# Two bottleneck layers in fp32: order of work at the two borders, in the middle stage and at the ends of the fused stage

## The chip, the cores and the metric

The kernel runs on one core of one Trainium2 chip. The metric is the device time of one execution in microseconds (us), as the median of several runs. One execution is profiled as well; its time is given beside the others.

## The reference

Two layers of the same form follow each other, on x of 64 x 1024 x 14 x 14 in fp32. Each is a bottleneck of three convolutions (1024 to 256 channels by 1x1, 256 to 256 by 3x3, 256 to 1024 by 1x1), each followed by a batch norm with the statistics of the batch, and closed by a scaled residual and a relu:

```python
def _bn(x, gamma, beta):
    mean = jnp.mean(x, axis=(0, 2, 3), keepdims=True)
    var = jnp.var(x, axis=(0, 2, 3), keepdims=True)
    xn = (x - mean) * jax.lax.rsqrt(var + EPS)
    return gamma.reshape(1, -1, 1, 1) * xn + beta.reshape(1, -1, 1, 1)

def layer(x, w1, b1, g1, be1, w2, b2, g2, be2, w3, b3, g3, be3, residual_scale):
    out = jax.nn.relu(_bn(_conv(x, w1, b1, 1, 0), g1, be1))
    out = jax.nn.relu(_bn(_conv(out, w2, b2, 1, 1), g2, be2))
    out = _bn(_conv(out, w3, b3, 1, 0), g3, be3)
    out = jax.nn.softplus(residual_scale)[0] * out
    return jax.nn.relu(x + out)
```

The second layer takes the first one's result.

## The kernel before

**Tiles.** The 64 images are cut into T = 32 tiles of two images, 392 columns each (`PX`). Channels lie on the 128 partitions: a tile of x has 8 slots (`CS`), a tile of the 256 inner channels has 2 (`MS`).

**Products.** A 1x1 convolution is cut into 2 x 2 blocks and done with seven products instead of eight (class `Seven`, with `Conv1`, `Conv3` and `Direct` for the three uses). `p1` to `p7` are the products on TensorE, and `after1` to `after7` what ScalarE and VectorE do with each. The products of one unit run between those of its neighbours (`stream`, `direct_stream`). `p4` is added onto the bank of `p1`, `p6` and `p7`, once ScalarE has copied it (`au<-ay`); `p5` and `p3` share a bank. The 3x3 convolution takes the rows and columns of the image through small transforms, so that TensorE sees the products `m<-sums`, `l<-diffs`, `columns<-sums` and `columns<-v`.

**Stages**, as the timeline shows them: conv1 of layer 0 until about 300 us, a border, conv2 of layer 0 until 580, a middle stage ("mixed") until 790, the fused stage until 1234, a border, conv2 of layer 1 until 1500, statistics (gram) until 1565, and the final stage until the end.

**Border.** A batch norm needs the statistics of all tiles, so the last results of conv1, the scale and shift, the norm of the first image rows and the first transform of conv2 follow each other. `Conv1.closing` writes this order by hand. The border of layer 0 has two tiles left in it (`two_tiles`), that of layer 1 one. `border.steps(n)` issues the next n steps of `first_combination` for slot 1 and then slot 0: on VectorE `r<-t` (line 854), `sums<-r` (782), `diffs<-r` (804) and `v<-r` (796), on ScalarE the edge copies of v; after them `steps<-y` (884) serves the next transform. `border.affine_of` makes `mv`, `minus`, the reciprocal, scale and shift.

**Mixed.** It computes conv3 of layer 0 for the statistics and keeps the results of the later tiles, unscaled, as z. `first()` does one tile in eight single products; after them `direct_stream` runs 60 units of seven products. In one step of a unit stands one product of its own or of the unit before. The results of a unit's second row are `kept<-cp,cu` (618, of `p7`) and `kept<-cy,kept` (612, of `p3`), and `finish` takes the second row's `bn_stats` (626) and stores z by SyncE's queue. Beside this, the inner tensor is normed (ScalarE, 128x320 columns at a time), centered (VectorE, `y<-y,minus_c`, 1506), and moved ("home", SyncE's queue) into another layout, in five pieces; the tables `moves` and the conditions on `unit` set when.

**Fused.** conv3 of layer 0 for half of the tiles and conv1 of layer 1 run between each other. For the other half (odd places p) `kept_rows` loads rows of z, scales them and adds them to x: on VectorE in one instruction (`x<-y,scale,x` or `x<-whole,scale,x`, 1906), or on GpSimd in two (1892 and 1893). A relu on ScalarE follows each row, and a store of the whole tile the last (`rest`). The last place, p = 31, stands right before the border of layer 1. `begun` is the list of what is left over from the tile before: two relus and the store of that tile.

**Order.** Instructions run in each engine's order of issue, which the hand-written loops set. DMAs are issued by SyncE (SP), ScalarE (ACT) and GpSimd (POOL), each with a queue of its own.

Of the kernel before, what the change touches and what calls it, by code (L numbers as in the profile page):

```python
# [18 lines left out]
CS = C // P  # L19
# [22 lines left out]
ROWS = 5 * CS, 13 * CS  # L42
AHEAD = 8


# [24 lines left out]
def bottlenecks(ctx: ExitStack, tc: tile.TileContext, x, w1s, w2s, w3s, pars, out):  # L70
# [272 lines left out]
    class Conv1(Seven):  # L343
# [34 lines left out]
        def bank(self, tag):  # L378

            if self.border is not None and tag == "x":  # L380
                return self.psum.tile(self.n, "ap" if len(self.ts) > 1 else "cx")
            return self.psum.tile(self.n, self.prefix + ("y" if self.border is not None and tag == "p" else tag))

# [7 lines left out]
        def closing(self, before):  # L391

            border = self.border

            yield from self.p1()
            for s in range(MS):
                summarize(self.stats[:, s : s + 1], T // 2 - 1, T - 2 * len(self.ts), PX)
            yield from before.p4()  # L400
            yield from self.p6()
            yield from self.p5()
            yield from self.p7()

            two_tiles = len(self.ts) > 1
            between = itertools.chain(*((before.p3(), before.p2()) if two_tiles else (before.p2(), before.p3())))
            yield from itertools.islice(between, CS // 4)
            yield from self.p4()
            border.affine_of(1)
            border.norm(1)  # L410
            yield from between
            border.begin()
            border.steps(3)
            if two_tiles:
                border.steps(2)
                yield from self.p2()
                border.steps(2)
                yield from self.p3()
            else:
                yield from self.p2()  # L420
                yield from self.p3()
            border.affine_of(0, lambda: border.steps(1 if two_tiles else 2))
            border.norm(0)
            border.steps(1 if two_tiles else 4)

# [202 lines left out]
    def direct_stream(units, between, finish):  # L628
# [3 lines left out]
        for k, now in enumerate(units):  # L632
            old = before and (before.p3, before.p7, before.p4)
            for step, part in enumerate((now.p1, *(old or (None, None))[:2], now.p5, now.p2, now.p6, old and old[2])):
                if step == 1 and earlier is not None:
                    earlier.finish()
                if part:
                    for _ in part():
                        pass
                if step == 2 and before is not None:  # L640
                    before.stat(0)
                yield k, step
# [66 lines left out]
    def conv2(b, par, aff, early, rest):  # L709
# [120 lines left out]
        def first_combination(x, s, t):  # L830
# [8 lines left out]
            for tiles in slice(0, 2), slice(2, full):  # L839
                run(stt(t[:, tiles], two_rows(0, s)[:, tiles, 0], -4.0, two_rows(0, s)[:, tiles, 1]))  # L840
            yield
            run(nc.vector.tensor_add(ra, t1, t2))
# [14 lines left out]
            yield  # L857
            x.subtract_columns(slice(1, 2), here)
            yield
            x.step_columns(slice(1, 2), here)  # L860
            yield

# [627 lines left out]
    def mixed(psum, pool, one, x_right, x_left, aff, minus_c, w3, made_c, summed_c, summed_a, mv3, xs, coming_x):  # L1490
# [92 lines left out]
        def first():  # L1583
# [8 lines left out]
            for i, (q, row) in enumerate(itertools.product(range(CS // 2), range(2))):  # L1592
# [9 lines left out]
                if i == 0:  # L1602
                    for _ in itertools.chain(summed_c, prepare(t + 1), itertools.islice(coming[t + 2], MS)):
                        pass
                if 1 < i < 6:
                    next(norms)
# [49 lines left out]
        moves = {}  # L1656
        for k, begin in enumerate((3, 13, 20, 28), 1):
            for i in range(8):
                moves[begin + i] = moves.get(begin + i, ()) + ((k, i // 2, (i % 2 * 2, i % 2 * 2 + 1)),)
        at = list(range(9, 48, 3))  # L1660
        at_first, _ = beds((None, None))
# [26 lines left out]
        for unit, step in stream:  # L1688
# [8 lines left out]
            if step == 3:  # L1697
                if q < 2 and t + 1 < T:
                    next(coming[t + 1], None)
                if 0 < unit <= 32 and unit % 2 == 0:  # L1700
                    center((unit - 1) // 8 + 1, (unit - 1) % 8 // 2)
                for where in moves.get(unit, ()):
# [91 lines left out]
    def residual(psum, xt, b, t, w3, aff, made=(), later=None):  # L1794
# [4 lines left out]
        for o in range(CS):  # L1799
# [10 lines left out]
            if (o + 1) % step == 0:  # L1810
                queue = nc.scalar if o + 1 == CS and (tail or b == 0) else nc.gpsimd if step == CS else nc.sync
                store = partial(
# [35 lines left out]
    def fused(psum, pool, one, right, coming, xs, raw, w1, w3, aff, par, stats, border, begun):  # L1848
# [34 lines left out]
        def kept_rows():  # L1883
# [13 lines left out]
            for r, (p, o) in enumerate(itertools.product(range(1, T, 2), range(CS))):  # L1897
# [3 lines left out]
                v, z = row(r, p, o)  # L1901
                if o % 2 and (p, o) not in ((T - 1, CS - 3), (T - 1, CS - 1)):
                    if p > 1 or o == CS - 1:
# [5 lines left out]
                later.append(partial(rest, v, p, o))  # L1909
                if len(later) > 2:  # L1910
                    later.pop(0)()
# [7 lines left out]
        def rest(v, p, o):  # L1919
            act(v, v, AF.Relu, bias=shift[:, o : o + 1])  # L1920
            if o == CS - 1:
                nc.scalar.dma_start(out=mids[places[p]], in_=xs[p].rearrange("p s f -> p (s f)"))

        whole = []
        pinned.append(True)
        a, c, rows = stream(first_convs(), T), stream(last_convs(), (KEPT - 1) * CS // 2), kept_rows()
        done, ended = LAG, None
        for i in range(LAG):
            next(c)
            if i == 2:  # L1930
                for late in begun:
                    late()
            if i % 2 == 1:
                next(rows)
        for k in itertools.count():
# [9 lines left out]
            late = k - 28 * (T - 4)  # L1945
            if (late >= 30 and late % 5 == 0) if late >= 20 else k % 7 == 3:
                next(rows, None)
# [333 lines left out]
```

## Time and profile before

| | before |
|---|---|
| median of 3 runs | 1893.97 us (1893.84 to 1894.53) |
| profiled execution | 1893.4 us |
| its span | 1891.4 us |
| TensorE, busy | 1872.2 us, 99% |
| VectorE, busy | 1575.9 us, 83% |
| ScalarE, busy | 1098.2 us, 58% |
| GpSimd, busy | 741.9 us, 39% |
| HBM | 228 GB/s over the span |

In timeline rows stand the start, the duration, the engine, the line, the operation with what it writes and reads, the count, and in brackets how long the engine was idle before it and what ended that. PE is TensorE, PEld its weight load, DVE VectorE, ACT ScalarE, POOL GpSimd, SP SyncE. In rows of waits stand who waited, for whom, the total, the number of times and the longest. Where a tile's name has a number (x_31), it tells which tile.

### The profile page before, as it was taken

What the parts mean: (1) busy time and instruction counts of PE and PEld (TensorE: products, weight loads), DVE (VectorE), ACT (ScalarE), POOL (GpSimd) and SP (SyncE); (2) the same over time, 40 slices, a digit from 0 to 9 for tenths busy, and PEclk for the clock granted to TensorE, in tenths of its full rate; (3) what the DMA queues carried; (4) which work ended last, traced back from release to release, by engine and by line L of the source; (5) the groups of instructions that cost most, each with busy time, mean ns of one, the idle gap of its engine ahead of it and who ended that gap; (6) DMA issues with size and microseconds to landing.
All of it is one profiled execution on the core that took longest, in us unless ns stands there. A gap on an engine that the chain in (4) does not pass through costs nothing.

```text
span 1891.4 us, 28568 instructions
## 1 busy us (share of the span) xinstructions
PE 1872.2 (99%) x9772; PEld 1560.4 (83%) x9772; DVE 1575.9 (83%) x2488; ACT 1098.2 (58%) x2287; POOL 741.9 (39%) x758
## 2 busy tenths in 40 slices
PE   9999999999999999999999999999999999999999
PEld 5555557999997998899999999989999987555555
DVE  5787867999998777788878788799999986888886
ACT  2222214677777665555555555457777792666666
POOL 0111100221205645377776776401121151666665
PEclk9999999999999999999999999999999999999999
DMA  7777644797865555778778899458788467799997
GB/s 288 272 252 271 216 181 138 203 219 214 207 205 160 181 175 206 252 270 310 271 282 309 284 299 285 195 171 222 211 208 226 143 161 292 263 341 336 358 344 271
DMA packets 262369, 458.19 MB, mean 242 GB/s; under 512 B 59152, under 2 KB 228976, under 8 KB 249040
## 3 DMA queue, kind: packets, MB, share of 16 engines
q1 hardware_dynamic: 224160, 373.28, 59.1%
q0 software_dynamic: 31216, 28.81, 7.9%
q10 hardware_dynamic: 6848, 54.28, 7.1%
q8 instruction: 78, 1.28, 0.3%
q14 instruction: 67, 0.55, 0.1%
HBM read 289.44 MB, written 141.03 MB: 228 GB/s over the span
## 4 chain that ended last, share of the span: by engine, by line
PE 91%; DVE 4%; ACT 2%; DMA 1%; issue 1%; POOL 1%; ACTq 0%; DVEq 0%; POOLq 0%
PE ay L159 20%; PE cy L159 16%; PE columns L159 13%; PE ap L159 11%; PE cp L159 10%; PE m L159 6%; PE l L159 6%; PE cx L159 5%; PE ax L159 4%; PE ps L159 1%; DMA w<-in_w 1%; ACT y L334 0%; ACT kept L334 0%; DVE y L751 0%; DVE f L1003 0%
## 5 line engine op out<-in xcount | busy, mean ns | idle before, releaser
L334 ACT ACTIVATE x<-x,shift 128x392 f32<-128x392 f32 x452 | 260.1, 614 | 79.0 <-DVE x L535 31.7
L159 PE MATMUL columns<-v,ub 128*128 128x224 f32 (+1 forms) x1536 | 302.7, 338 | 1.3 <-ACT columns L334 0.8
L159 PEld LDWEIGHTS columns<-v,ub 128*128 128x128 f32 x1536 | 268.6, 188 | 7.7 <-ACT columns L334 1.5
L334 ACT ACTIVATE cu<-cy,scale 128x196 f32<-128x196 f32 (+1 forms) x360 | 175.7, 500 | 166.6 <-PE cy L159 159.2
L159 PE MATMUL ay<-at,ws 128*128 128x196 f32 (+1 forms) x768 | 192.6, 382 | 0.5 <-ACT y L334 0.5
L159 PEld LDWEIGHTS ay<-at,ws 128*128 128x128 f32 x768 | 136.2, 190 | 35.3 <-issue 0.7
L535 DVE SCALAR_TENSOR_TENSOR x<-cp,scale,x 128x196 f32<-128x196 f32 (+1 forms) x240 | 124.6, 519 | 46.0 <-PE cp L159 44.5
L666 POOL TENSOR_TENSOR x<-x,cu 128x392 f32<-128x392 f32 x120 | 125.6, 1048 | 73.2 <-DVE x L535 72.3
L334 ACT ACTIVATE au<-ay 128x196 f32<-128x196 f32 (+1 forms) x139 | 53.6, 386 | 169.6 <-PE ay L159 158.3
L159 PE MATMUL l<-diffs,ub 128*128 128x224 f32 (+1 forms) x768 | 149.6, 337 | 0.3 <-issue 0.3
L159 PE MATMUL m<-sums,ua 128*128 128x224 f32 (+1 forms) x752 | 146.0, 336 | 0.4 <-issue 0.2
L159 PEld LDWEIGHTS l<-diffs,ub 128*128 128x128 f32 x768 | 134.6, 189 | 1.3 <-issue 0.7
L1104 POOL DMA_DIRECT2D y<-f x24 | 32.2, 1644 | 257.3 <-DVE f L1003 257.3
L159 PEld LDWEIGHTS m<-sums,ua 128*128 128x128 f32 x752 | 131.4, 189 | 1.7 <-issue 0.6
L558 POOL TENSOR_TENSOR x<-x,cu 128x196 f32<-128x196 f32 (+1 forms) x120 | 105.0, 875 | 47.5 <-ACT cu L334 19.8
L159 PE MATMUL cx<-y,w 128*128 128x196 f32 (+1 forms) x396 | 122.2, 394 | 1.1 <-ACT cx L334 1.1
L159 PE MATMUL cy<-y,w 128*128 128x196 f32 (+1 forms) x374 | 117.2, 401 | 0.9 <-DVE y L1570 0.8
L563 POOL TENSOR_TENSOR x<-x,cu 128x392 f32<-128x392 f32 x60 | 79.4, 1323 | 85.2 <-DVE x L535 80.9
L334 ACT ACTIVATE y<-y,shift,scale 128x320 f32<-128x320 f32 (+9 forms) x98 | 107.8, 1121 | 8.3 <-DVE shift L2033 7.0
L206 POOL DMA_DIRECT2D u<-y x48 | 26.0, 544 | 211.1 <-ACT y L334 210.4
L1892 POOL TENSOR_SCALAR y<-y,scale 128x392 f32<-128x392 f32 x57 | 92.4, 1621 | 29.0 <-DVE scale L2224 28.2
L626 DVE BATCH_NORM_STATS2 stats<-kept 128x6 f32<-128x392 f32 x120 | 67.4, 562 | 42.8 <-ACT kept L334 41.5
(314 smaller groups left out, 4556.8 us busy)
## 6 DMA issues: line engine op xcount, KB each, us to landing
ub<-u SPq DMA_DIRECT2D x92, 768.0 KB, 5.6
x<-in_x SPq DMA_DIRECT2D x35, 1568.0 KB, 8.5
mid<-x ACTq DMA_DIRECT2D x32, 1568.0 KB, 8.3
x<-mid SPq DMA_DIRECT2D x32, 1568.0 KB, 8.9
out<-x SPq DMA_DIRECT2D x123, 392.0 KB, 7.1
x<-in_x SPq DMA_DIRECT2D x108, 392.0 KB, 7.8
ua<-u SPq DMA_DIRECT2D x92, 256.0 KB, 3.2
z<-kept SPq DMA_DIRECT2D x60, 392.0 KB, 2.9
```

Of the source, the lines that this page charges most:

```text
L159: tc.keep_in_program_order(nc.tensor.matmul(*args, **kw))
L206: nc.gpsimd.dma_start(out=us[b][i][:, s, o], in_=u)
L334: tc.keep_in_program_order(nc.scalar.activation(*args, **kw))
L535: run(nc.vector.scalar_tensor_tensor(v, bank, self.scale[:, o : o + 1], v, ALU.mult, ALU.add))
L558: run(nc.gpsimd.tensor_add(self.part(1, 1), self.part(1, 1), u3))
L563: run(nc.gpsimd.tensor_add(v, v, self.u12))
L626: run(nc.vector.bn_stats(self.stats[:, self.o[row], self.t - KEPT, :], self.z[:, row]))
L666: nc.gpsimd.tensor_add(v, v, self.u12[:, i * self.n : (i + 1) * self.n])
L1104: nc.gpsimd.dma_start(out=out_rows[3][:, o], in_=fa[:, o, :full], accum_op=ALU.add)
L1892: run(nc.gpsimd.tensor_scalar(z, z, scale[:, o : o + 1], None, ALU.mult))
```

## The change

It reorders work at five places and changes no arithmetic.

1. *Border of both layers.* The second half of slot 1's first combination (`r<-t`, `sums<-r`, and what follows) comes behind shift instead of ahead of the last result. Between `minus` and the reciprocal only one step is left or none; the last `v<-r` of slot 1 is done together with that of slot 0, and `diffs<-r` of slot 1 between the two `steps<-y` of slot 0.
2. *Border of layer 1.* The fifth product has its own bank (cp) in place of one of y's, and the fourth product comes directly behind the seventh, where four matmuls of `ax` stood between.
3. *Mixed.* One of the four norm pairs of `first()`, with its centers and moves, goes into the stream's units 1 to 4, and later norms and centers shift by one pair. `finish` (the second row's `bn_stats` and the store of z) moves from step 1 to step 3, behind the two results of that row.
4. *Start of fused.* The two leftover relus are issued apart, and the store goes from ScalarE's queue to SyncE's.
5. *End of fused.* The rows of p = 31 follow a table of times; row 3 goes from GpSimd to VectorE, three rows come ahead of a sum, and the last tile's store is cut in two.

The diff, cut to its core:

```diff
+ROW_TIMES = 30, 35, 40, 46, 46, 46, 49, 51, 53, 55, 57, 58, 61, 65, 67
...
-            if self.border is not None and tag == "x":
-                return self.psum.tile(self.n, "ap" if len(self.ts) > 1 else "cx")
-            return self.psum.tile(self.n, self.prefix + ("y" if self.border is not None and tag == "p" else tag))
+            if self.border is not None and tag in "xp":
+                own = dict(x="ap", p="ay") if len(self.ts) > 1 else dict(x="cx", p="cp")
+                return self.psum.tile(self.n, own[tag])
+            return self.psum.tile(self.n, self.prefix + tag)
...
-            yield from itertools.islice(between, CS // 4)
+            if two_tiles:
+                yield from itertools.islice(between, CS // 4)
             yield from self.p4()
             border.affine_of(1)
             border.norm(1)
             yield from between
             border.begin()
-            border.steps(3)
-            if two_tiles:
-                border.steps(2)
-                yield from self.p2()
-                border.steps(2)
-                yield from self.p3()
-            else:
-                yield from self.p2()
-                yield from self.p3()
-            border.affine_of(0, lambda: border.steps(1 if two_tiles else 2))
+            border.steps(5 if two_tiles else 3)
+            yield from self.p2()
+            yield from self.p3()
+            border.affine_of(0, lambda: border.steps(0 if two_tiles else 1))
             border.norm(0)
-            border.steps(1 if two_tiles else 4)
+            border.steps(2 if two_tiles else 3)
...
-                if step == 1 and earlier is not None:
+                if step == 3 and earlier is not None:
                     earlier.finish()
...
                 run(stt(t[:, tiles], two_rows(0, s)[:, tiles, 0], -4.0, two_rows(0, s)[:, tiles, 1]))
+                if s == 0 and tiles.start == 0:
+                    x.subtract_columns(slice(1, 2), slice(1, 2))
...
-            x.subtract_columns(slice(1, 2), here)
-            yield
-            x.step_columns(slice(1, 2), here)
-            yield
+            if s == 0:
+                x.subtract_columns(slice(1, 2), here)
+                x.step_columns(slice(1, 2))
...
-                if 1 < i < 6:
+                if 1 < i < 5:
                     next(norms)
...
-        for k, begin in enumerate((3, 13, 20, 28), 1):
+        for k, begin in enumerate((5, 13, 20, 28), 1):
...
+        for i in range(2):
+            moves[3 + i] = ((0, 3, (i * 2, i * 2 + 1)),)
...
-                if 0 < unit <= 32 and unit % 2 == 0:
-                    center((unit - 1) // 8 + 1, (unit - 1) % 8 // 2)
+                if 0 < unit <= 34 and unit % 2 == 0:
+                    center((unit + 5) // 8, (unit + 5) % 8 // 2)
...
-                queue = nc.scalar if o + 1 == CS and (tail or b == 0) else nc.gpsimd if step == CS else nc.sync
+                queue = nc.scalar if o + 1 == CS and tail else nc.gpsimd if step == CS and b else nc.sync
...
-                if o % 2 and (p, o) not in ((T - 1, CS - 3), (T - 1, CS - 1)):
+                if (p, o) == (T - 1, CS - 2):
+                    while later:
+                        later.pop(0)()
+                        yield
+                if o % 2 and (p < T - 1 or o < 3):
...
-                if len(later) > 2:
+                if len(later) > 2 and (p < T - 1 or o < 3):
                     later.pop(0)()
...
             if i == 2:
-                for late in begun:
-                    late()
+                begun.pop(0)()
+            if i == 4:
+                while begun:
+                    begun.pop(0)()
...
-            if (late >= 30 and late % 5 == 0) if late >= 20 else k % 7 == 3:
+            for _ in range(at_end[late] if late >= 20 else k % 7 == 3):
                 next(rows, None)
```

In the border of layer 0, VectorE had this order at the last result (`y<-ay`; `au_1282` is its copy by ScalarE), with slot 1's sums ahead of it and `diffs<-r` between `minus` and the reciprocal:

```order
L437 SCALAR_TENSOR_TENSOR y<-ap,par_161,au_1246 128x14x28
L440 BN_STATS stats_0_128<-y 128x6
L854 TENSOR_TENSOR r<-t 128x448
L782 TENSOR_TENSOR sums<-r 128x224
L437 SCALAR_TENSOR_TENSOR y<-ay,par_161,au_1282 128x14x28
L440 BN_STATS stats_0_128<-y 128x6
L1985 BN_AGGR mv<-stats_0_128 128x2
L2002 TENSOR_SCALAR v<-mv 128x1
L2011 TENSOR_SCALAR minus<-mv 128x1
L804 TENSOR_TENSOR diffs<-r 128x224
```

Now it has this one there:

```order
L434 SCALAR_TENSOR_TENSOR y<-ay,par_161,au_1282 128x14x28
L437 BN_STATS stats_0_128<-y 128x6
L1995 BN_AGGR mv<-stats_0_128 128x2
L2012 TENSOR_SCALAR v<-mv 128x1
L2021 TENSOR_SCALAR minus<-mv 128x1
L2023 RECIPROCAL r<-sd 128x1
L2033 SCALAR_TENSOR_TENSOR q<-v,r 128x1
L2034 TENSOR_TENSOR rg<-r,par_161 128x1
L2035 SCALAR_TENSOR_TENSOR scale<-q,rg 128x1
L2043 SCALAR_TENSOR_TENSOR shift<-scale,minus,par_161 128x1
L853 TENSOR_TENSOR r<-t 128x448
L779 TENSOR_TENSOR sums<-r 128x224
```

`r<-t` and `sums<-r` moved from two rows ahead of `y<-ay` to behind shift; `diffs<-r` lies further on.

In a unit of mixed's stream, VectorE had the second row's statistics between the center pair and the two results:

```order
L1298 STREAM_TRANSPOSE zt_3625<-home 128x2x256
L1506 TENSOR_SCALAR y<-y,minus_c 128x320 x2
L626 BN_STATS stats_3507<-kept 128x6
L618 TENSOR_TENSOR kept<-cp,cu_4159 128x196
L612 TENSOR_TENSOR kept<-cy,kept 128x196
L626 BN_STATS stats_3507<-kept 128x6
L1298 STREAM_TRANSPOSE zt_3623<-home 128x2x256
```

Now both rows' statistics stand together, behind the results:

```order
L1296 STREAM_TRANSPOSE zt_3613<-home 128x2x256
L1504 TENSOR_SCALAR y<-y,minus_c 128x320 x2
L615 TENSOR_TENSOR kept<-cp,cu_4089 128x196
L609 TENSOR_TENSOR kept<-cy,kept 128x196
L623 BN_STATS stats_3504<-kept 128x6 x2
L615 TENSOR_TENSOR kept<-ay,cu_4118 128x196
L609 TENSOR_TENSOR kept<-ay,kept 128x196
L623 BN_STATS stats_3504<-kept 128x6 x2
L1296 STREAM_TRANSPOSE zt_3614<-home 128x2x256
```

The first `bn_stats` of each unit (of the row before) moved past the results of lines 618 and 612 (now 615 and 609).

At the end of fused, VectorE had two rows of x_31 behind the sums of x_15, and one more behind the statistics:

```order
L437 SCALAR_TENSOR_TENSOR y<-ax,par_163,au_9094 128x7x28
L454 TENSOR_TENSOR at_9172<-x_15_8817 128x784
L437 SCALAR_TENSOR_TENSOR y<-ap,par_163,au_9168 128x7x28
L456 TENSOR_TENSOR at_9171<-at_9172,x_15_8817 128x784
L457 TENSOR_TENSOR at_9170<-x_15_8817 128x784
L1906 SCALAR_TENSOR_TENSOR x_31_8939<-whole,scale,x_31_8939 128x392 x2
L440 BN_STATS stats_1_5568<-y 128x6
L1906 SCALAR_TENSOR_TENSOR x_31_8939<-whole,scale,x_31_8939 128x392
L437 SCALAR_TENSOR_TENSOR y<-ap,par_163,au_9140 128x7x28
L1970 BN_AGGR part<-stats_1_5568 128x2
```

Now three stand ahead of the sums, and one behind:

```order
L434 SCALAR_TENSOR_TENSOR y<-ax,par_163,au_9091 128x7x28
L1910 SCALAR_TENSOR_TENSOR x_31_8936<-whole,scale,x_31_8936 128x392 x3
L451 TENSOR_TENSOR at_9169<-x_15_8814 128x784
L434 SCALAR_TENSOR_TENSOR y<-ap,par_163,au_9165 128x7x28
L453 TENSOR_TENSOR at_9168<-at_9169,x_15_8814 128x784
L454 TENSOR_TENSOR at_9167<-x_15_8814 128x784
L437 BN_STATS stats_1_5565<-y 128x6
L1910 SCALAR_TENSOR_TENSOR x_31_8936<-whole,scale,x_31_8936 128x392
L434 SCALAR_TENSOR_TENSOR y<-ap,par_163,au_9137 128x7x28
L1980 BN_AGGR part<-stats_1_5565 128x2
```

Two rows of x_31 fewer stand between the sums and the second `y<-ap`, and GpSimd's two instructions for row 3 are gone.

More of the change, by code (lines that the diff above doesn't have):

```diff
@@ L1920, in rest @@
             act(v, v, AF.Relu, bias=shift[:, o : o + 1])
-            if o == CS - 1:
-                nc.scalar.dma_start(out=mids[places[p]], in_=xs[p].rearrange("p s f -> p (s f)"))
+            a = (0, CS - 2)[p == T - 1 and o == CS - 1]
+            if o == CS - 1 or p == T - 1 and o == CS - 3:
+                nc.scalar.dma_start(
+                    out=mids[places[p]][:, a * PX : (o + 1) * PX], in_=xs[p][:, a : o + 1].rearrange("p s f -> p (s f)")
+                )
         whole = []
@@ L1927, in fused @@
         done, ended = LAG, None
+        at_end = collections.Counter(ROW_TIMES)
         for i in range(LAG):
```

## The prediction

> **What bounds the kernel now.** I read the page first, then the chain of waits, then who keeps PE waiting, then the timeline at each place that the diff touches.
>
> ```profile
> span 1891.4 us, 28568 instructions
> PE 1872.2 (99%) x9772; PEld 1560.4 (83%) x9772; DVE 1575.9 (83%) x2488; ACT 1098.2 (58%) x2287; POOL 741.9 (39%) x758
> PE 91%; DVE 4%; ACT 2%; DMA 1%; issue 1%; POOL 1%; ACTq 0%; DVEq 0%; POOLq 0%
> ```
>
> PE is busy for 99% of the span and carries 91% of the chain. The change removes no matmul, so all it can win is PE's waiting; the rest of the span is fixed. Where PE waits at the places touched stands in the waits of PE, grouped by who ends them (total us, times, longest), and in the waiters of line 612:
>
> ```profile
> PE columns L159 <- DVE sums L782: 3.2, 3, 1.7
> PE cy L159 <- DVE kept L612: 2.0, 3, 0.7
> PE cy L159 <- ACT cu L334: 1.3, 3, 0.9
> PE cx L159 <- ACT cx L334: 1.1, 1, 1.1
> PE ap L159 <- DVE y L437: 1.1, 1, 1.1
>   PEld cy L159: 1.8, 4
> ```
>
> 3.2 + 2.0 + 1.3 + 1.1 + 1.1 = 8.7 us, and 1.8 of weight loads, is nearly all there is to win. The sum is made against the profiled execution, 1893.4 us: a span of 1891.4 and 2.0 around it. The median of the runs, 1893.97, lies 0.57 above it.
>
> **Border of layer 0 (two tiles).** The timeline between conv1 and conv2:
>
> ```profile
> 301.11 2.80 PE L159 MATMUL ay<-x,ws 128*128 128x392 f32 x8
> 303.72 0.61 DVE L854 TENSOR_TENSOR r<-t 128x448 f32<-128x448 f32 x1
> 304.67 0.62 DVE L437 SCALAR_TENSOR_TENSOR y<-ay,par,au 128x392 f32<-128x392 f32 x1
> 311.33 1.78 PE L159 MATMUL columns<-sums,ua 128*128 128x224 f32 x8 [1.72 <-DVE sums L782]
> 313.23 0.55 DVE L796 TENSOR_TENSOR v<-r 128x384 f32<-128x384 f32 x1
> 313.70 2.95 DVE L884 TENSOR_TENSOR steps<-y 128x2688 f32<-128x2688 f32 x1
> 319.33 1.41 PE L159 MATMUL m<-sums,ua 128*128 128x168 f32 x8 [0.20 <-DVE sums L782]
> 320.96 1.35 DVE L796 TENSOR_TENSOR v<-r 128x1152 f32<-128x1152 f32 x1
> ```
>
> The last result, y<-ay, starts at 304.67 though its product ends at 303.91, because r<-t and sums<-r of slot 1 stand ahead of it on DVE. Behind it follow the last statistics, scale, shift, the norm and the sums for which PE waits 1.72. With the two moved behind shift this chain starts about 304.0, 0.67 earlier; diffs, which also leaves it, may bring 0.2 more: columns come 0.7 to 0.9 earlier. What is late next is DVE itself: PE already waits 0.20 for DVE's sums at 319.33, behind the long steps<-y, which starts only when v is done. The merged v (128x768) lies between the 0.55 of 384 and the 1.35 of 1152 elements, midway 0.95, so 0.4 of the gain is paid back there: 0.5 (bounds 0 and 0.9). Below nothing it cannot well go: the 0.61 of r<-t that now lies behind shift is less than the wait that the move shortens, 1.72, and lies beside ACT's norm there.
>
> **Start of mixed.**
>
> ```profile
> 595.08 1.20 ACT L334 ACTIVATE y<-y,shift,scale 128x320 f32<-128x320 f32 x2 [0.60 <-ACT kept L334]
> 597.02 0.57 PE L159 MATMUL cx<-y,w 128*128 128x196 f32 x2 [1.11 <-ACT cx L334]
> ```
>
> The last norm pair occupies ACT for 1.20 right ahead of the evictions for which PE then waits 1.11. It goes to the stream's units 1 and 2, with its centers on DVE and four moves on SP's queue behind it. What it hid is then late by the evictions' own pace: I take 0.9 (0 to 1.1).
>
> **The stream.** The second row's bn_stats and the store of z move from ahead of the last two results of a unit to behind them.
>
> ```profile
> 643.79 1.31 DVE L1506 TENSOR_SCALAR y<-y,minus_c 128x320 f32<-128x320 f32 x2
> 645.03 0.56 DVE L626 BATCH_NORM_STATS2 stats<-kept 128x6 f32<-128x392 f32 x1
> 645.51 0.34 DVE L618 TENSOR_TENSOR kept<-cp,cu 128x196 f32<-128x196 f32 x1
> 645.77 0.35 DVE L612 TENSOR_TENSOR kept<-cy,kept 128x196 f32<-128x196 f32 x1
> 646.26 0.57 PE L159 MATMUL cy<-ct,w 128*128 128x196 f32 x2 [0.66 <-DVE kept L612]
> 663.71 0.64 DVE L1506 TENSOR_SCALAR y<-y,minus_c 128x320 f32<-128x320 f32 x2
> ```
>
> In this unit DVE's center pair, the statistics (0.48 from start to start) and the two results stand in a row, and PE waits 0.66 for the second. Without the statistics in the row the wait shrinks by 0.48. There are three such waits (2.0 together): 1.4. The four weight loads held by line 612 (1.8) give about 0.2 each by the same shift: 0.8. Sum 2.2; upper bound 2.0 + 1.8 = 3.8, lower 0, if the statistics merely delay the next row. The norm and center that the units gain lie beside PE, and cost at most one more wait of 0.66. The z store goes later by two steps on SP, past the loads for the tiles and ahead of the moves of the same unit; these move copies that are read several units later, and no wait in the rows names them, so I price it at nothing; if they were late, transposes on DVE would be, and then gram's products at the stream's end.
>
> **Start of fused.** Timeline, and the DMA issues between 792 and 794 (KB each, us to landing):
>
> ```profile
> 792.05 1.12 ACT L334 ACTIVATE x<-x,shift 128x392 f32<-128x392 f32 x2
> 793.59 0.42 ACT L334 ACTIVATE cu<-cy,scale 128x196 f32<-128x196 f32 x1 [0.41 <-ACT x L334]
> 794.07 0.60 PE L159 MATMUL cy<-y,wt 128*128 128x196 f32 x2 [0.93 <-ACT cu L334]
> mid<-x ACTq DMA_DIRECT2D x1, 1568.0 KB, 11.5
> y<-z SPq DMA_DIRECT2D x2, 196.0 KB, 12.4
> 805.22 0.63 DVE L1906 SCALAR_TENSOR_TENSOR x<-y,scale,x 128x392 f32<-128x392 f32 x1 [2.86 <-DMA y<-z]
> ```
>
> Two relus and the issue of a store stand on ACT ahead of the cu that PE waits 0.93 for. One relu of the two (0.56) and the issue leave: cu about 0.75 earlier, and PE with it (0.3 to 0.93). The store now stands in SP's queue, behind two y<-z loads and ahead of six more row loads: that is a rival, below.
>
> **End of fused and border of layer 1.**
>
> ```profile
> 1207.44 1.05 DVE L1906 SCALAR_TENSOR_TENSOR x<-whole,scale,x 128x392 f32<-128x392 f32 x1
> 1210.63 0.98 DVE L454 TENSOR_TENSOR at<-x 128x784 f32<-128x784 f32 x1 [1.80 <-POOL whole L1892]
> 1214.12 1.15 DVE L1906 SCALAR_TENSOR_TENSOR x<-whole,scale,x 128x392 f32<-128x392 f32 x2
> 1216.20 0.41 DVE L437 SCALAR_TENSOR_TENSOR y<-ap,par,au 128x196 f32<-128x196 f32 x1
> 1216.66 1.59 PE L159 MATMUL ap<-at,ws 128*128 128x196 f32 x8 [1.09 <-DVE y L437]
> 1222.69 4.22 PE L159 MATMUL ay<-at,ws 128*128 128x196 f32 x24 [0.45 <-ACT y L334]
> 1227.41 1.52 PE L159 MATMUL ay<-at,w 128*128 128x196 f32 x8
> 1235.18 1.78 PE L159 MATMUL columns<-sums,ua 128*128 128x224 f32 x8 [0.86 <-DVE sums L782]
> ```
>
> Two last rows of 0.58 stand ahead of y<-ap (1216.20), for which PE waits 1.09. Three rows now come before at<-x, in DVE's idle 1.80: at 0.58 each they are 1.7 and fit; at the 1.05 of the row at 1207.44 they would spill 1.35. y<-ap then comes 1.15 earlier and PE's 1.09 goes: I take 1.1. Of the 0.45 at 1222.69 some 0.2 goes by the same shift. The fourth product stands directly behind the seventh and waits for ACT's copy of its bank; it starts near 1227.4 as before, and PE is idle there for as long as the half of ax took that now moves behind it, at most 0.76 by the 1.52 of eight matmuls. Behind the waiting product on PE stand the products of ax and ap; they end later by that much, but nobody waits for them at that moment: PE itself waits 0.86 for sums at 1235.18 anyway, which covers it. Without that cover it would cost the 0.76. Fewer DVE steps ahead of the reciprocal take about 0.25 from that. Sum 1.55; lower bound 0.1, where the rows spill; upper 1.09 + 0.45 + 0.86 = 2.4. The fifth product's own bank and the split last store lie in no wait shown: 0.
>
> **Sum.** 0.5 + 0.9 + 2.2 + 0.75 + 1.55 = 5.9. Profiled execution 1887.5; with the 0.57, 1888.1. About 0.2% (3.8 us) is what a measurement can tell from no change, so below 1890.2 is faster and above 1897.8 slower.
>
> **Rivals.**
>
> *Every wait goes.* If each bound is reached, 0.9 + 1.1 + 3.8 + 0.93 + 2.4 = 9.1: 1884.9. For it: the waits are short and the moved work is longer than most of them. Against: at 319.33 and 1235.18 the next wait already stands behind.
>
> *The statistics bring nothing.* bn_stats keeps DVE as busy; if the following unit's results wait for it, 2.2 falls away: gain 3.7, 1890.3, no difference. The stretch 643.79 to 646 with no idle DVE speaks for it, the 0.64 center pair at 663.71, with slack, against.
>
> *The store holds up the rows.* A store that took 11.5 us beside other queues now stands ahead of six row loads in one queue, and DVE takes rows in order. DVE has already stood 2.86 at 805.22 for a row, and PE shows no wait there, so that much is free. At the page's mean rate
>
> ```profile
> DMA packets 262369, 458.19 MB, mean 242 GB/s; under 512 B 59152, under 2 KB 228976, under 8 KB 249040
> ```
>
> 1568 KB are 6.6 us; less 2.86 leaves 3.8 for PE: gain 2.1, 1891.9, no difference. The Trainium skill ("DMA: Bandwidth & Descriptors", Queues, rings and completion order) says that each DMA engine takes turns between the queue rows for which it has work, and drains each row's own ring: by it the store on its own queue shared the engines with the row loads, and in theirs it goes first. No run here shows this yet.
>
> *Slower: center pairs beside POOL.* The pair at 643.79 took 1.31, the one at 663.71 0.64. With statistics behind the results and the norms two units later, all 17 pairs that the stream then has (at its even units up to 34) could meet POOL's work and make PE wait 0.66 each: 11.2 less the 2.0 that is there, 9.2 more, and the other 3.7 still won: 5.5 slower, 1899.5. Slower begins at 7.5 us of new waits, 11 to 12 pairs more. Against: most pairs in before stand in no PE wait, as only three waits are there. The Trainium skill ("SBUF — State Buffer", Who interferes with whom) says that VectorE and GpSimd share a port pair, held for a whole instruction, and that tensor_scalar can enter a mode that takes it; the 1.31 against 0.64 agrees.
>
> **How the numbers follow.** The forecast, a gain of 4.0 to 7.5 (1886.5 to 1890.0), 0.62; every wait goes 0.10; statistics nothing 0.12; store 0.07; pairs 0.09. Faster 0.62 + 0.10 = 0.72, same 0.12 + 0.07 = 0.19, slower 0.09. The range takes in all but the last: 1884.9 to 1892.1.
>
> **What would show it.** The waits <- kept L612 shrink from 2.0 to under 0.7, columns' longest from 1.7 to near 1, the 1.11 before cx, the 1.09 before ap go, cu's 0.9 falls under 0.3. Wrong: DVE waiting over 2.86 for y<-z behind the store; a wait of PE above 1.1 before the fourth product of layer 1's border; or PE's total busy time differing by over 1 us, since I take matmuls as unchanged.

## The result, and the profile after

| | before | changed |
|---|---|---|
| median of 9 runs | 1894.01 us (1893.38 to 1894.74) | 1889.31 us (1888.26 to 1890.46) |
| ratio, 95% interval | | 0.9975 (0.9965 to 0.9985) |
| profiled execution, span | 1893.4, 1891.4 us | 1888.93, 1886.9 us |

The change gains 4.7 us by the medians and 4.5 by the spans; forecast were 5.9. The page of the changed kernel, and its largest waits of PE:

```profile
span 1886.9 us, 28576 instructions
PE 1872.4 (99%) x9772; PEld 1560.3 (83%) x9772; DVE 1574.3 (83%) x2487; ACT 1098.9 (58%) x2283; POOL 739.5 (39%) x756
PE cy L160 <- DVE kept L609: 1.1, 2, 0.9
PE cy L160 <- ACT cu L335: 0.8, 4, 0.2
PE ay L160 <- ACT au L335: 0.6, 2, 0.4
PE columns L160 <- DVE sums L779: 0.6, 2, 0.4
PE m L160 <- DVE sums L779: 0.6, 1, 0.6
```

PE's work is the same (1872.2 before, 1872.4 now); waiting is what went. `kept L609` is what was `kept L612`: 2.0 in three waits became 1.1 in two, but the longest grew from 0.7 to 0.9. The waits for cx (1.1) and before ap (1.1) are gone.

To see where, the start of one matmul is compared with the start of the same matmul before. The timeline of the changed kernel, PE:

```profile
27.11 2.80 PE L160 MATMUL ay<-x,w 128*128 128x392 f32 x8
310.31 1.78 PE L160 MATMUL columns<-sums,ua 128*128 128x224 f32 x8 [0.42 <-DVE sums L779]
318.70 1.41 PE L160 MATMUL m<-sums,ua 128*128 128x168 f32 x8 [0.60 <-DVE sums L779]
446.76 1.79 PE L160 MATMUL columns<-v,ub 128*128 128x224 f32 x8 [0.23 <-ACT columns L959]
595.50 0.57 PE L160 MATMUL cx<-y,w 128*128 128x196 f32 x2
597.29 0.60 PE L160 MATMUL cy<-ct,wt 128*128 128x196 f32 x2 [0.23 <-ACT cu L335]
644.25 0.57 PE L160 MATMUL cy<-ct,w 128*128 128x196 f32 x2 [0.24 <-DVE kept L609]
682.78 0.57 PE L160 MATMUL cy<-ct,w 128*128 128x196 f32 x2 [0.20 <-POOL y L1568]
737.00 0.60 PE L160 MATMUL cy<-ct,w 128*128 128x196 f32 x2 [0.88 <-DVE kept L609]
790.01 0.60 PE L160 MATMUL cy<-y,wt 128*128 128x196 f32 x2 [0.18 <-ACT cu L335]
791.13 0.60 PE L160 MATMUL cy<-y,wt 128*128 128x196 f32 x2 [0.18 <-ACT cu L335]
1192.54 0.49 PE L160 MATMUL cp<-ct,wt 128*128 128x196 f32 x2
1212.30 1.55 PE L160 MATMUL ap<-at,ws 128*128 128x196 f32 x8
1222.68 1.59 PE L160 MATMUL ay<-at,w 128*128 128x196 f32 x8 [0.42 <-ACT au L335]
1230.54 1.78 PE L160 MATMUL columns<-sums,ua 128*128 128x224 f32 x8 [0.20 <-DVE sums L779]
1245.64 1.38 PE L160 MATMUL m<-sums,ua 128*128 128x168 f32 x8 [0.65 <-issue]
```

and the rows of before that belong to them and have not been shown:

```profile
27.25 2.80 PE L159 MATMUL ay<-x,w 128*128 128x392 f32 x8
447.20 1.80 PE L159 MATMUL columns<-v,ub 128*128 128x224 f32 x8 [0.23 <-ACT columns L961]
598.72 0.60 PE L159 MATMUL cy<-ct,wt 128*128 128x196 f32 x2
685.32 0.57 PE L159 MATMUL cy<-ct,w 128*128 128x196 f32 x2 [0.62 <-DVE kept L612]
739.30 0.60 PE L159 MATMUL cy<-ct,w 128*128 128x196 f32 x2 [0.67 <-DVE kept L612]
792.21 0.60 PE L159 MATMUL cy<-y,wt 128*128 128x196 f32 x2 [0.18 <-ACT cu L334]
1195.65 0.49 PE L159 MATMUL cp<-ct,wt 128*128 128x196 f32 x2
1250.36 1.38 PE L159 MATMUL m<-sums,ua 128*128 128x168 f32 x8 [0.24 <-issue]
```

Read against each other: at 27 us, ahead of every edited place, PE is already 0.14 us earlier (27.25 to 27.11); this comes out of the first loads and not out of the change. PE is 1.02 earlier at columns (311.33 to 310.31), 0.63 at the next wait (319.33 to 318.70), and keeps 0.44 (447.20 to 446.76). At the start of mixed, 1.52 (597.02 to 595.50) and 1.43 (598.72 to 597.29). In the stream 2.01 (646.26), 2.54 (685.32), then **less**, 2.30 (739.30), and 2.20 at its end (792.21). At the start of fused 2.94 (794.07 to 791.13), before the border of layer 1 3.11, at ap 4.36, behind the border 4.72. The end, 4.5, is 0.2 less.

| place | forecast | PE's gain by the trace |
|---|---|---|
| first loads, not edited | | 0.14 |
| border of layer 0 | 0.5 | 0.44 - 0.14 = 0.30 (right behind it 0.63 - 0.14 = 0.49) |
| start of mixed | 0.9 | 1.43 - 0.44 = 0.99 |
| stream | 2.2 | 2.20 - 1.43 = 0.77 |
| start of fused | 0.75 | 2.94 - 2.20 = 0.74 |
| end of fused and border of layer 1 | 1.55 | 4.72 - 3.11 = 1.61 |
| sum | 5.9 | 4.5 (with +0.17 in fused and -0.2 in the last stages) |

### The profile page after: what moved, and what is told of

Its sections match the earlier page's. It is cut to its first block, busy times and chain, and to the rows that moved or that the text cites. A ratio compares the mean times of both kernels' runs of the same rounds, so it can differ in the third digit from the quotient of the medians.

```text
span 1886.9 us, 28576 instructions
## 1 busy us (share of the span) xinstructions
PE 1872.4 (99%) x9772; PEld 1560.3 (83%) x9772; DVE 1574.3 (83%) x2487; ACT 1098.9 (58%) x2283; POOL 739.5 (39%) x756
## 4 chain that ended last, share of the span: by engine, by line
PE 91%; DVE 3%; issue 2%; ACT 1%; DMA 1%; POOL 0%; SPq 0%; ACTq 0%; DVEq 0%; POOLq 0%
PE ay L160 20%; PE cy L160 16%; PE columns L160 12%; PE ap L160 11%; PE cp L160 10%; PE m L160 6%; PE l L160 6%; PE cx L160 5%; PE ax L160 4%; PE ps L160 1%; DMA y<-f 0%; ACT y L335 0%; DVE f L1001 0%; DMA x<-in_x 0%; DVE v L793 0%
## 5 line engine op out<-in xcount | busy, mean ns | idle before, releaser
L961 ACT ACTIVATE columns<-m 128x448 f32<-128x448 f32 (+1 forms) x144 | 70.8, 492 | 55.3 <-PE m L160 48.4
```

What stands on the lines that cost most here:

```text
L961: copy(v, m, AF.Copy)
```

## The experiments

Each kernel is the changed one with one edit; after_again has none, border_mean and pair_mean have two. The table gives, for the same matmul, its start less its start in the profile of the changed kernel shown above (positive: later), at seven marks of that profile, and the median of the runs.

| kernel | 27 | 447 | 597 | 683 | 737 | 790 | 1511 | median us |
|---|---|---|---|---|---|---|---|---|
| rows_back | +0.25 | +0.03 | +0.02 | +0.05 | +0.05 | +0.05 | +1.59 | 1889.78 |
| store_act | +0.62 | +0.71 | +0.72 | +0.41 | +0.08 | +0.08 | +1.36 | 1889.88 |
| relus_together | +0.25 | -0.04 | -0.05 | -0.04 | -0.03 | -0.03 | +0.24 | 1889.04 |
| p4_back | +0.11 | +0.09 | +0.09 | +0.09 | +0.09 | +0.09 | +0.02 | 1888.72 |
| border_back | +0.04 | +0.50 | +0.40 | +0.36 | -0.32 | -0.33 | -0.36 | 1887.84 |
| pair_back | -0.24 | +0.19 | +1.17 | +0.87 | +0.27 | +0.27 | +0.42 | 1889.14 |
| stats_back | +0.07 | -0.24 | -0.25 | +0.79 | +0.69 | +0.57 | +0.55 | 1889.42 |
| stats_held | +0.66 | +0.82 | +0.81 | +0.81 | +0.13 | +0.60 | +0.54 | 1888.62 |
| after_again | +0.01 | -0.18 | -0.18 | -0.48 | -0.46 | -0.46 | -0.51 | 1888.81 |
| mean_late | +1.78 | +1.51 | +1.50 | +1.20 | +0.16 | +0.24 | +0.21 | 1888.55 |
| border_mean | +0.14 | +0.23 | +0.14 | +0.10 | -0.95 | -1.11 | -1.07 | 1888.10 |
| pair_mean | +0.11 | -0.20 | +0.79 | +0.50 | -0.57 | -0.57 | -0.39 | 1889.42 |

after_again is the changed kernel once more. Its median is 0.5 below the first, and its profile drifts by 0.3 between 597 and 683 us, by 0.17 near 356 us and by 0.4 in the last stages. Near 356 us, in conv2 of layer 0, kernels that are edited only elsewhere shift too (relus_together, mean_late and pair_mean by 0.25 to 0.3 earlier, pair_back by 0.25 later). mean_late is 1.78 late at 27 us, in the first loads, which its edit does not touch. So medians decide nothing under about 1 us here, and of the trace only a step of over 0.3 at the edited place counts.

**Last rows.**

```diff
-            for _ in range(at_end[late] if late >= 20 else k % 7 == 3):
+            if (late >= 30 and late % 5 == 0) if late >= 20 else k % 7 == 3:
...
-                if o % 2 and (p < T - 1 or o < 3):
+                if o % 2 and (p, o) not in ((T - 1, CS - 3), (T - 1, CS - 1)):
...
```

> The changed kernel with the last rows at their old times, row 3 on GpSimd again and the last store in one piece; the border's order stays the changed one. My theory, two rows of 0.58 stood ahead of the result for which PE waited 1.09: PE's wait before ap comes back, 1.1 to 1.25 us late at that place and, since VectorE's cover of 0.86 before columns is gone, as much at the end: near 1890.5. Rival, the border's order alone made that gain: under 0.3 late before ap, time near 1889.5.

Measured: 1889.78 us (1889.14 to 1890.46). PE is 0.04 late at 798 us, 1.30 late at ap and 1.58 late at 1218, and keeps it: what was expected at ap, and 0.28 more behind it. The wait is back, with VectorE's rows ahead of it, in the timeline of rows_back:

```profile
1207.56 0.97 DVE L451 TENSOR_TENSOR at<-x 128x784 f32<-128x784 f32 x1 [1.80 <-POOL whole L1892]
1211.06 1.15 DVE L1906 SCALAR_TENSOR_TENSOR x<-whole,scale,x 128x392 f32<-128x392 f32 x2
1213.60 1.59 PE L160 MATMUL ap<-at,ws 128*128 128x196 f32 x8 [1.08 <-DVE y L434]
```

In the changed kernel the three rows fill that idle time and end with it:

```profile
1205.64 2.12 DVE L1910 SCALAR_TENSOR_TENSOR x<-whole,scale,x 128x392 f32<-128x392 f32 x3
1207.68 0.96 DVE L451 TENSOR_TENSOR at<-x 128x784 f32<-128x784 f32 x1
```

The rows, with the store in two pieces that goes with them, are worth 1.54, nearly all of the 1.61 at this place.

**The fourth product's place.**

```diff
-            if two_tiles:
-                yield from itertools.islice(between, CS // 4)
+            yield from itertools.islice(between, CS // 4)
```

> The changed kernel with four matmuls of ax again between the seventh and the fourth product at the border of layer 1. My theory: the four matmuls fill PE's wait of 0.42 for au, but the fourth product comes 0.2 to 0.4 later and with it the last result, scale, shift and sums, so that columns is 0.2 to 0.4 later: 1889.5 to 1889.7. Rival, the fill is worth more than the later product: PE's wait for au goes and columns starts no later, time lower by up to 0.4.

Measured: 1888.72 us (1887.92 to 1889.28); +0.09 at 798 us, +0.05 at 1218 and 1245. The longest wait for sums before columns is 0.9 again, where the changed kernel waits 0.42 for au and 0.20 for sums. PE waits at one place or at the other, and neither theory has its gain.

**Leftover relus and store.** store_act gives the store back to ScalarE's queue; relus_together issues both relus and the store at once again, with the store in SyncE's queue.

```diff
 # store_act
-queue = nc.scalar if o + 1 == CS and tail else nc.gpsimd if step == CS and b else nc.sync
+queue = nc.scalar if o + 1 == CS and (tail or b == 0) else nc.gpsimd if step == CS else nc.sync
 # relus_together
-                begun.pop(0)()
-            if i == 4:
                 while begun:
                     begun.pop(0)()
```

> The changed kernel with the store of the tile before fused back in ScalarE's queue, behind the second relu, which stays apart. My theory, the relu and the issue of the DMA each held ScalarE: the issue of about 0.34 us is back ahead of a cu and PE loses 0.1 to 0.35 at 793 us; VectorE's wait for y<-z goes from 0.6 back towards 2.9 us without PE losing by it: 1889.4 to 1889.7. Rival, the queue holds up the row loads: with the store out of SyncE's queue the rows land earlier, VectorE's wait for y<-z falls to nothing, and the time is 0.3 us or more lower.

> The changed kernel with the leftover relus and the store issued together again at the start of fused, the store in SyncE's queue. My theory: the second relu, 0.56 us, stands ahead of cu again and PE loses 0.4 to 0.6 of the 0.75 won at 793 us: near 1889.8. Rival, only the DMA's issue on ScalarE had cost: PE not late, time unchanged.

Measured: 1889.88 us (1888.56 to 1891.78) and 1889.04 (1888.41 to 1890.22). At 791 to 793 us the store's issue costs PE 0.23, as expected, and the second relu 0.2, where 0.4 to 0.6 were expected. Together this is 0.43 of the 0.74 won there; where the rest comes from, neither run shows. What I had not expected comes after. VectorE's wait for the row, in the changed kernel and then in store_act, with PE's wait behind it:

```profile
799.79 1.43 DVE L1910 SCALAR_TENSOR_TENSOR x<-y,scale,x 128x392 f32<-128x392 f32 x1 [0.56 <-DMA y<-z]
```

```profile
803.54 0.63 DVE L1910 SCALAR_TENSOR_TENSOR x<-y,scale,x 128x392 f32<-128x392 f32 x1 [3.64 <-DMA y<-z]
806.16 0.60 PE L160 MATMUL cp<-y,wt 128*128 128x196 f32 x2 [0.35 <-DVE x L532]
```

With the store in a queue of its own, the row comes 3.7 us later (799.79 to 803.54), and PE, 0.28 late at 798 us, is 1.35 late at 1218. It loses 0.98 of this over the matmuls from 798.64 to 805.27 us. The kernel before, with the store in ScalarE's queue as well, is later there by only 0.12 more (2.72 to 2.84), although VectorE waits 2.86: so the SyncE queue keeps the changed kernel from losing about 1, and adds little to what it gains over the kernel before. Why the kernel before does not lose it was not tried. So my theory had the wait right and its cost wrong (PE loses by it), and the rival had the queue's effect the wrong way round.

**Border order.** border_back takes back the order of steps at both borders, and nothing else.

```diff
...
-            if s == 0:
-                x.subtract_columns(slice(1, 2), here)
-                x.step_columns(slice(1, 2))
+            x.subtract_columns(slice(1, 2), here)
+            yield
+            x.step_columns(slice(1, 2), here)
+            yield
...
-            border.steps(5 if two_tiles else 3)
+            border.steps(3)
+            if two_tiles:
+                border.steps(2)
...
```

> The changed kernel with the old order of steps on VectorE and ScalarE at both borders (second half of slot 1's combination ahead of the last result); PE's order and the banks stay the changed ones. My theory: at the border of layer 0 columns starts 1.0 us later, of which 0.45 remains behind the border; at the border of layer 1 the wait before columns grows from 0.20 by 0.3 to 0.7, of which under 0.2 remains; time near 1889.9. Rival, the next wait gives all of it back: columns late by 1.0 and conv2 not late at all, time unchanged at both.

Measured: 1887.84 us (1887.55 to 1888.49), the lowest median of all, against 1889.9 expected. At its places the trace is as expected: +0.92 at columns, +0.50 at 447 us; at the border of layer 1 -0.38 at the first columns, +0.09 at the second (1237 us), -0.31 behind: 0.47 are lost for a moment and 0.07 remain. But near 737 us it is suddenly ahead by 0.32.

**Norm pair.**

```diff
-                if 1 < i < 5:
+                if 1 < i < 6:
...
```

> The changed kernel with the fourth norm pair, its centers and its moves back in first(). My theory, ScalarE's 1.20 us pair stood right ahead of the evictions for which PE waited 1.1: that wait comes back, PE is 1.0 us later at the start of the stream, and the time near 1890.3. Rival, PE caught it up in the stream: late by 1.0 at 600 us and by under 0.3 at 790 us, time unchanged.

Measured: 1889.14 us (1888.76 to 1889.83). The wait of 1.11 for cx is back and PE 0.98 later at 597 us (+0.19 to +1.17). At 737 us 0.6 of that is given back: the rival is right in part, and at one place.

**Statistics.**

```diff
-                if step == 3 and earlier is not None:
+                if step == 1 and earlier is not None:
```

> The changed kernel with finish (second row's statistics and store of z) back at step 1 of the unit. My theory, that the statistics cost the results their 0.48 where the row on VectorE is dense and delay the chain g, product home at the stream's end: PE loses about 0.5 each at the two places near 644 and 683 us and wins back about 0.2 near 737, so the stream is 0.7 to 0.8 us longer and the time near 1890.1. Forecast's own term, 2.2 from the statistics: 1891.5. Rival, statistics bring nothing: the same time, 1889.3, and PE's starts shifted by under 0.2 at the end of the stream.

Measured: 1889.42 us (1889.12 to 1890.13). PE goes from -0.26 at 608 us to +0.26 at 644 and +0.79 at 683, then back to +0.57 at 790: 0.83 for the whole stream. By the trace the theory holds, and the forecast's 2.2 does not.

**What stands at 737 us.** Three kernels in which PE came later to this place (border_back, pair_back, store_act) made up some of it there, or all. The timeline of VectorE and GpSimd just ahead, in the changed kernel:

```profile
732.57 1.02 DVE L623 BATCH_NORM_STATS2 stats<-kept 128x6 f32<-128x392 f32 x2
733.61 1.54 DVE L1744 TENSOR_TENSOR g<-ap,by 64x65 f32<-64x65 f32 x5
735.15 1.59 POOL L1568 TENSOR_SCALAR y<-y,minus_c 128x392 f32<-128x392 f32 x1
735.19 1.10 DVE L1763 TENSOR_SCALAR home<-w,g 128x1024 f32<-128x1024 f32 x1
736.32 0.36 DVE L615 TENSOR_TENSOR kept<-ay,cu 128x196 f32<-128x196 f32 x1
736.60 0.35 DVE L609 TENSOR_TENSOR kept<-cy,kept 128x196 f32<-128x196 f32 x1
```

in the kernel before, VectorE alone:

```profile
734.84 0.56 DVE L626 BATCH_NORM_STATS2 stats<-kept 128x6 f32<-128x392 f32 x1
735.42 1.55 DVE L1744 TENSOR_TENSOR g<-ap,by 64x65 f32<-64x65 f32 x5
736.99 1.12 DVE L1763 TENSOR_SCALAR home<-w,g 128x1024 f32<-128x1024 f32 x1
738.04 0.55 DVE L626 BATCH_NORM_STATS2 stats<-kept 128x6 f32<-128x392 f32 x1
738.90 0.35 DVE L612 TENSOR_TENSOR kept<-cy,kept 128x196 f32<-128x196 f32 x1
```

and in border_back:

```profile
735.20 0.76 DVE L1768 TENSOR_SCALAR home<-w,g 128x1024 f32<-128x1024 f32 x1
735.52 1.90 POOL L1573 TENSOR_SCALAR y<-y,minus_c 128x392 f32<-128x392 f32 x1
```

PE's result (609) stands behind a product of weights and means (home, 128x1024) that follows g, the end of the gram statistics. The moved statistics stand ahead of g, two in a row now, where the kernel before has one ahead of g (734.84) and one behind the product (738.04): in both, two of them stand ahead of the result. And the product takes 1.10 where GpSimd's operation started 0.04 ahead of it, 0.76 where it started 0.32 behind; there GpSimd takes 1.90 in place of 1.59. In border_back PE came 0.36 later to this place, but VectorE's product starts at the same time in both (735.20 against 735.19): this much is absorbed, and the shorter product wins 0.34 more. Two edits went at this place. stats_held holds one bn_stats back by a unit; mean_late moves the two products into VectorE's idle time near 749 and 756 us.

```diff
 # stats_held
-                    earlier.finish()
+                    if k == 46:
+                        held.stat(1)
+                    earlier.finish(k != 45)
+                    held = earlier
...
 # mean_late (for the stream alone)
+        beside = tags[0] == "ax"
+        if not beside:
...
+            if beside and h == 1:
+                run(nc.vector.scalar_tensor_tensor(by_mean, w[1], means[1], by_mean, ALU.mult, ALU.add))
             matmul(t1, g0[:, right], w3[:, 0, cols, :], start=True, stop=False)
             yield
+            if beside and h == 0:
+                run(nc.vector.tensor_scalar(by_mean, w[0], means[0], None, ALU.mult))
```

> The changed kernel with one bn_stats (unit 45's second row of the unit two before) held back by one unit, behind the first multiplication of the chain g, product home. My theory, this chain starts 0.48 earlier: PE's wait of 0.88 near 737 us shrinks to about 0.4, the next unit's results may give up to 0.48 back: time 0 to 0.5 lower, 1888.8 to 1889.3. Rival, the wait is set by PE's gram product or by ScalarE: the 0.88 stays.

> The changed kernel itself, as the measure for the runs beside it: 1889.3, with PE's wait of 0.9 near 737 us.

> The changed kernel with the two products of weights and means (128x1024, home) that stand on VectorE behind g near 735 and 738 us put into VectorE's idle time near 749 and 756 us; the end of layer 1's statistics is left as it was. My theory, that this chain sets PE's start near 737 us and that it gave back there what other kernels had lost before: the 0.88 goes, PE is 0.6 to 0.9 us earlier from there to 790 us, and the time 0.6 to 0.9 below the changed kernel's. Rival, the next results on VectorE are late instead: a wait of 0.5 or more near 740 or 750 us, time unchanged.

> The old order of steps at the borders together with the late products of means. My theory, that the old border order came out lower in time only because its later PE met the chain near 737 us in a better phase: with that chain out of the way its 0.5 us from the border of layer 0 stays to the end, and it is 0.3 to 0.6 slower than the late products of means alone. Rival, the old border order is itself better: 0.3 us or more faster than the late products of means alone.

> The fourth norm pair back in first() together with the late products of means. My theory: the 1.0 us that the pair costs PE at 597 us is no longer given back near 737 us, PE is 0.8 to 1.0 later at 790 us than with the late products of means alone, and the time 0.8 to 1.0 higher. Rival, it is caught up elsewhere: late by under 0.3 at 790 us.

Measured: stats_held 1888.62 us (1887.85 to 1889.65). Its wait falls from 0.88 to 0.19 (0.23 of this is the product, 0.87 here in place of 1.10), but the next unit waits 0.55; PE wins 0.68 and gives 0.47 back. mean_late 1888.55 us (1887.66 to 1889.08) beside 1888.81 (1887.62 to 1890.86) of the changed kernel: by the trace it wins 0.96 from 683 to 790 us (+1.20 to +0.24) and the wait at 737 us is gone; by time the two are not told apart. border_mean and pair_mean, with the same late products, win 1.21 and 1.07 in that stretch.

pair_mean: the pair costs 0.99 at 597 us (-0.20 to +0.79), and at 790 us it is 0.90 behind mean_late once their difference at 447 us is taken off (-0.57 + 0.20 against 0.24 - 1.51): the chain near 737 had hidden the pair's loss. Its time is 0.87 above mean_late, as expected, though that is within what medians scatter. border_mean (1888.10 us, 1887.58 to 1888.66) was expected 0.3 to 0.6 above mean_late and came out 0.45 below, which is what the rival said. By its trace the old border order is still the later one at its place: right behind the border, at 318.70 us, it has +0.48 once its 27 us mark is taken off, as border_back has, and mean_late has nothing. Why both kernels with the old order have low medians is open. Of the changed kernel's 18 runs (both series), 5 lie as low as the highest of the 12 with the old order (1888.66): the new border order starts PE earlier at its place, but that it gains time is not shown.

Apart from this open point, no version is shown to beat the changed kernel in time.

## Why the prediction was right, by its steps

The gain of 4.7 by the medians lies in the range of 4.0 to 7.5, but 1.2 below the forecast's 5.9 and only 1.0 above the 3.7 of the rival in which the statistics bring nothing. One term of the sum accounts for the difference: with the 0.77 that the stream gave in place of 2.2, the sum is 4.5.

**What bounds the kernel.** Right: no matmul went, PE's busy time differs by 0.2, and by the trace 4.4 of the gain lies at the five places.

**Border of layer 0.** 0.5 forecast; 0.49 right behind the border and 0.30 at 447 us in the trace, where the 0.14 of the first loads is taken off; 0.48 lost by the old order at 318.70 (border_back and border_mean). The rest of the way to 447 us shifts by as much in kernels that leave the border alone. The payback was foreseen at the right place: the wait at 319.33 grew from 0.20 to 0.60, and the 0.88 won at columns (1.02 less 0.14) lies in the 0.7 to 0.9. Whether it shows in the time of the runs is open, as said above.

**Start of mixed.** 0.9 forecast, 0.99 in the trace, 0.98 by pair_back. What the forecast lacked is that such a gain can be lost again at the next place where VectorE leads.

**The stream.** This is the step that failed: 2.2 forecast, 0.77 measured in the trace, 0.83 by undoing it alone. The shift of 0.48 was right at two of the three waits (0.66 to 0.24, 0.62 to 0.20). The third I took for the same kind from its row in the waits, without its neighbours: there the statistics moved from behind the product to ahead of the chain of g, both ahead of the result, and the wait grew, 0.67 to 0.88. So kept L612's 2.0 became 1.1, not the under 0.7 that I had named as a sign; the other waits named went or shrank as said or more, and none of the signs of being wrong came. The 0.8 for the weight loads was not there either: line 609 holds 1.6 of cy and 1.0 of ay, where 612 held 1.8 and 0.6.

**Start of fused.** 0.75 forecast, 0.74 measured. But the store's queue, which I counted as a rival that loses 3.8, works the other way: ScalarE's would cost the changed kernel about 1.1. The rule of the Trainium skill ("DMA: Bandwidth & Descriptors", Queues, rings and completion order) that I read as speaking for that rival speaks against it: a store in its own queue takes turns with the row loads on each DMA engine, while behind the two first loads in theirs it can't. The rows agree, with 3.64 of waiting against 0.56. For the loads behind the store I read it rightly, but VectorE never waits for one of them.

**End of fused and border of layer 1.** 1.55 forecast, 1.61 measured, by other parts: I had 1.3 for the rows (1.1 and 0.2), which bring 1.54, the fourth product's place and the border's order nothing that the trace can tell. My 0.25 for fewer steps ahead of the reciprocal was not there. The fifth product's bank was not tried alone.

**The rivals.** Every wait goes: it would have needed 3.8 from the stream. Statistics bring nothing: refuted by the trace, which shows 0.83, though not by the time of stats_back, within what medians scatter. Center pairs beside POOL: they met it no more than before, with a mean of 471 ns in place of 529 for the 32 of 128x320:

```profile
L1506 DVE TENSOR_SCALAR y<-y,minus_c 128x320 f32<-128x320 f32 x32 | 15.6, 529 | 0.4 <-ACT y L334 0.4
L1504 DVE TENSOR_SCALAR y<-y,minus_c 128x320 f32<-128x320 f32 x32 | 13.7, 471 | 0.0
```

The mechanism is real all the same, at the 128x1024 product, and worth 0.34 there.

## What to carry to other kernels

A wait belongs to the whole row of work ahead of it: before a term of one instruction's length is counted at several waits, look at what stands ahead of each of them. Parts of a change do not add where a second engine leads: what PE wins before such a place is lost there, and taking one part back may cost nothing. Where a change is worth less than the runs scatter, compare the start of one and the same instruction on the bounding engine in two traces, take off what stood between them ahead of the first edited place, and run the same kernel twice to know how far that goes.

## What the runs showed of the hardware that I had not expected

A 1568 KB store in the queue of the 196 KB row loads, behind the first two of them, delayed VectorE less than in a queue of its own: VectorE waited between nothing and 0.8 for the row in the twelve kernels with the first (0.56 in the one shown), 3.64 and 2.86 in the two with the second (store_act and the kernel before).

VectorE and GpSimd slow each other, and which of them is slowed goes by who starts first. VectorE's 128x1024 tensor_scalar took 0.73 with nothing on GpSimd beside it (mean_late), and 1.10 where GpSimd's 128x392 operation had started 0.04 ahead; that operation then kept its 1.59. Where VectorE had started first, GpSimd took 1.90 (border_back) and 2.02 (pair_back). In store_act, where the two starts are 0.01 apart, it took 2.14:

```profile
735.60 2.14 POOL L1568 TENSOR_SCALAR y<-y,minus_c 128x392 f32<-128x392 f32 x1
735.61 0.75 DVE L1763 TENSOR_SCALAR home<-w,g 128x1024 f32<-128x1024 f32 x1
```

The Trainium skill ("SBUF — State Buffer", Who interferes with whom) says that whoever issues first has the shared pair for the whole instruction and the other blocks fully. The order agrees but for the 0.01 in store_act. The size nearly agrees for GpSimd: it lost 0.31, 0.43 and 0.55 where 0.44, 0.56 and 0.76 of VectorE's product were left when it started. It does not for VectorE, which lost under 0.4 of the 1.55 that GpSimd had left.
